# Exps of an attention stage moved to VectorE and GpSimd, and an earlier fetch of row maxima

## The chip, the core and the metric

The kernel runs on one NeuronCore of a Trainium2 chip. The core has five engines that run in parallel, each its own stream of instructions in order: TensorE (PE in the profile) multiplies matrices, with weight loads shown as PEld; ScalarE (ACT) evaluates functions such as exp; VectorE (DVE) does elementwise work and reductions; GpSimd (POOL) does elementwise work and issues some DMAs; SyncE (SP) issues DMAs alone. Operands lie in SBUF, 128 partitions wide; TensorE writes to PSUM, eight banks. Engines wait for each other on semaphores. The metric is device time in microseconds (us), lower is better.

## The reference, cut to what matters

Four graph layers on x (3327 x 128) and a 3327 x 3327 matrix adj, each of the form x = x + layer(relu(layernorm(x)), adj). The change is in layer 0, an attention with 128 heads of 8 elements each. Both encodings are adj, so that adj is added twice:

```python
q = (x @ Wq.T).reshape(d, n, h)          # d = 128 heads, n = 3327, h = 8
k = (x @ Wk.T).reshape(d, n, h)
v = (x @ Wv.T).reshape(d, n, h)
a = jnp.einsum('dnh,dmh->dnm', q, k) * scale
a = a + spatial_encoding + edge_encoding # both are adj
a = jax.nn.softmax(a, axis=2)
out = jnp.einsum('dnm,dmh->dnh', a, v)
```

There are 128 x 3327 x 3327 exps. The other three layers are products with adj or its transpose, with small elementwise work.

## The kernel before, in words

The attention stage takes the time from about 515 to 10,478 us of the profiled span. It holds the scores transposed: keys on partitions, queries along the free axis. The queries are cut into NC = 7 chunks of CW = 476 columns; the 128 heads into NG = 32 groups of four; the 3328 padded keys into NT = 26 tiles of 128, taken two at a time as NQ = 13 pairs (q = 0 to 12). One unit `u` is one (chunk, group, pair). Four heads of 26 tiles, less some hand work, are what a group asks of ScalarE.

A pair occupies two PSUM banks of the seven of `S`, one per tile (r = 0 "even" and r = 1 "odd"). `seed` (L660, VectorE) copies the half of the shifted adjacency that the pair needs into each bank. `scores` (L666, TensorE) then adds k.q of the first head, and for each next head k.q minus that of the head before, in place: adj and the shift are put in once for four heads. `exps` (L678 and L681, ScalarE) reads the bank after each head and writes exp(2 S) to SBUF tiles `e0` to `e3`. Where a pair's banks lie side by side, one ScalarE instruction takes both (952 columns, "wide", L678); in one pair of seven they don't, and two of 476 are used (L681). `values` (L719, TensorE) multiplies the exps by v, with a column of ones for the softmax's denominator, into the bank `po`, four heads side by side.

The order is written out by hand, in program order per engine, by the loop over slots `i`. A slot is one exp of one head of one pair; four slots make a unit, and heads are staggered: head j of unit u is in slot 4u + 3j. At odd slots TensorE gets the scores of the next two slots and then the value products of one tile of an earlier unit: the tile in place p of a group (0 to 25) comes in slot 2p + 11 from the group's start. `seed` of the odd bank comes at slots with i % 4 = 1, of the even bank at i % 4 = 2. After a bank's last exp, its next seed may start.

For pairs 0, 4 and 8 (`by_hand`), the second tile's exp of head 0 isn't ScalarE's: VectorE evaluates a polynomial (`hand_exp`, L692 to L703), in nine steps spread over four units by the queue `by_vector`. `heads_of` puts the result later into the order of the value products.

GpSimd, in order, does these in each group: the DMAs that store `po`'s copy (L727 on VectorE, L731 on GpSimd, in pair 2 or 3 of the next group), then at pair 4 the six negations of the next group's q (`negate_q`, L576), the copy of the next v (`spread_v`, L586) and a check copy `all_here` (L590). These wait for the next group's loads, which SP issues at pair 1: `load_qk` (L564, L566, L568; 40 DMAs) and `load_v` (L581).

Beside this runs the preparation of later chunks. Each 128 x 128 column block of adj ("square") is loaded in four parts, transposed by VectorE in two halves a part (`turn`, L293; at pairs 7 and 11), reduced to row maxima (`largest`, L297), gathered to DRAM (`gather`, L312, four small DMAs), fetched back in another layout (`back`, L317), combined by VectorE into a bound (`finish`, L321 to L323, at pair 7), stored (L300), and shifted on GpSimd by 13 subtractions (`shift`, L307), one a unit. A square takes seven groups: parts in the groups with g % 7 = 1 to 4, gather to spread in g % 7 = 5, shifts in 6 and 0. There are 22 such squares. `plan_squares` sets these units. SP executes gather, `back` and the loads in the order of the program; before, `back` comes at pair 3, after the loads.

The adjacency tiles of a chunk sit in the pool `e_adj` and those of the next are loaded during the last group of a chunk.

Of the kernel before, what the change touches and what calls it, by code (L numbers as in the profile page):

```python
# [10 lines left out]
F32 = mybir.dt.float32  # L11
# [4 lines left out]
I32 = mybir.dt.int32  # L16
AF = mybir.ActivationFunctionType
ALU = mybir.AluOpType
# [4 lines left out]
P = 128  # L23
N = 3327
D = 128
H = 8
HD = D * H
NT = 26
NP = NT * P
NQ = NT // 2  # L30
# [5 lines left out]
NC = 7  # L36
CW = 476
# [11 lines left out]
EXP_C = (753.2197875976562, 522.0919799804688, 180.93934631347656, 41.8090705871582, 7.287807941436768)  # L49
EXP_LAST = 0.0013276338577270508  # L50
EXP_BITS = 117 + 0.3594970703125
LOG2_E2 = 2.8853900817779268
EXP_LEAST = -110.0
# [27 lines left out]
def width_of(c):  # L81

    return min(CW, N + 1 - c * CW)
# [8 lines left out]
def gnn_kernel(ctx: ExitStack, tc: tile.TileContext, x, adj, Wq, Wk, Wv, Wo, embed, layer,  # L92
# [442 lines left out]

    with tc.tile_pool(name="e1", bufs=1) as e1, tc.tile_pool(name="e_adj", bufs=30) as e_adj, \
            tc.tile_pool(name="e2", bufs=2) as e2, tc.tile_pool(name="e_e", bufs=1) as e_e, \
            tc.tile_pool(name="e_t", bufs=1) as e_t, tc.tile_pool(name="e_h", bufs=1) as e_h, \  # L540
            tc.tile_pool(name="e_ps", bufs=1, space=PSUM) as e_ps:


# [71 lines left out]
        with tc.If(loose < 1), tc.manual_schedule():  # L615
# [10 lines left out]
            pairs = [(c, g, q) for c in range(NC) for g in range(NG) for q in range(NQ)]  # L626
            n = len(pairs)
            adj_of, shift_of, v_of, e_of, here = {}, {}, {}, {}, {}
            by_vector = deque()

# [23 lines left out]
            def bank(u, r):  # L654
                return S[:, banks(u)[r], :width_of(pairs[u][0])]
# [17 lines left out]
            def exps(u, j):  # L673
                w, (even, odd) = width_of(pairs[u][0]), banks(u)
                e = e_of[u, j] = e_e.tile([P, 2, CW], F32, name=f"e{j}", bufs=(5, 4, 3, 2)[j])
                hand = j == 0 and by_hand(u)
                if even > odd and not hand:
                    touch(u, (0, 1), nc.scalar.activation(e[:, :, :w], S[:, odd:even + 1, :w], AF.Exp, scale=2.0))  # L678
                    return
                for r in range(1 if hand else 2):  # L680
                    touch(u, [r], nc.scalar.activation(e[:, 1 - r, :w], bank(u, r), AF.Exp, scale=2.0))  # L681

            def by_hand(u):

                return 0 <= u < n and pairs[u][2] in (0, 4, 8)

            def hand_exp(u):

# [13 lines left out]
                yield  # L702
                nc.vector.scalar_tensor_tensor(e, e, EXP_C[0], power.bitcast(F32), op0=ALU.add, op1=ALU.mult)  # L703

            def heads_of(u, r):


                first = (u, r)
                if by_hand(u) and r == 1:
                    first = (u + 1, 0)  # L710
                elif by_hand(u - 1):
                    first = (u, 1) if r == 0 else (u - 1, 1)
                return [first] + [(u, r)] * 3

            def values(u, r):
                c, g, q = pairs[u]
                w, k = width_of(c), c * NG + g
                for j, (v, of) in enumerate(heads_of(u, r)):
                    nc.tensor.matmul(po[32 * j:32 * j + H + 1, :w], VA[k % 2][:, 2 * pairs[v][2] + of, j, :],  # L719
                                     e_of[v, j][:, 1 - of, :w], start=(q == 0 and r == 0),  # L720
                                     stop=(q == NQ - 1 and r == 1))

            def store(u):
                c, g, q = pairs[u]
# [8 lines left out]
            def loads(u):  # L733

                c, g, q = pairs[u]
                k = c * NG + g
                if k + 1 < NC * NG:
                    nxt = divmod(k + 1, NG)
                    if q == 1:
                        load_qk(*nxt)  # L740
                        v_of[k + 1] = load_v(*nxt)
                    if q == 4:
                        negate_q(*nxt)
                        spread_v(*nxt, v_of.pop(k + 1))
                        here[k + 1] = all_here(*nxt)
                if c + 1 < NC and (g, q) == (0, 0):
                    plan_squares(c)
                if g == NG - 1 and c + 1 < NC:
                    if q == 0:
                        shift_of[c + 1] = load_shift(c + 1)  # L750
                        adj_of[c + 1] = []
                    while len(adj_of[c + 1]) < min(NT, 2 * q + 6):
                        adj_of[c + 1].append(load_adj(c + 1, len(adj_of[c + 1]), shift_of[c + 1]))


# [2 lines left out]
            def plan(u, f, *a):  # L758
                behind.setdefault(u, []).append((f, a))

            def plan_squares(c):
                for k, s in enumerate(range(squares_of(c), squares_of(c + 1))):
                    sq, u = Square(e_t, s), (c * NG + 7 * k + 1) * NQ
                    for j in range(4):
                        plan(u, sq.load, j)
                        plan(u + 7, sq.turn, j, 0)
                        plan(u + 11, sq.turn, j, 1)
                        plan(u + 12, sq.largest, j)
                        u += NQ
                    for k, f in ((0, sq.gather), (3, sq.back), (7, sq.finish), (8, sq.store), (10, sq.spread)):  # L770
                        plan(u + k, f)
                    for k in range(NQ):
                        plan(u + NQ + 5 + k, sq.shift, 2 * k, 2 * k + 2)
                    plan(u + 2 * NQ + 6, sq.store, shifted_by_tile)
# [15 lines left out]
            for i in range(-4, 4 * n + 15):  # L790
                u, j = in_slot(i)
                if 0 <= u < n:
                    exps(u, j)
                at = i % 4
                if i == -4:
                    seed(0, 0)
                if at == 0 and by_hand(i // 4):
                    by_vector.append(hand_exp(i // 4))
                if at == 0 and by_vector:
                    for k in range(2 if by_hand(i // 4) else 3):  # L800
                        if by_vector and next(by_vector[0], True):
                            by_vector.popleft()
                if at == 0 and i > 0:
                    for f, a in behind.pop(i // 4, ()):
                        f(*a)
                if at == 1 and (i + 3) // 4 < n:
                    seed((i + 3) // 4, 1)
                u = (i - 14) // 4
                if at == 2 and 0 <= u < n and pairs[u][2] == NQ - 1:
                    store(u)  # L810
                if at == 2 and (i + 6) // 4 < n:
                    seed((i + 6) // 4, 0)
                if at % 2:
# [409 lines left out]
```

## Time and profile before

| What | Value |
|---|---|
| median of 3 runs | 11,431.28 us (11,428.13 to 11,438.58) |
| profiled execution: its time | 11,439.36 us |
| profiled execution: its span | 11,437.2 us |
| granted TensorE clock | 0.969 of full |
| busy in the stage (515.6 to 10,478 us, 9,962.4 us): TensorE, ScalarE | 9,783.0, 9,762.0 us |
| busy in the stage: VectorE, GpSimd | 7,634.5, 1,813.3 us |

The span is the time from the first to the last instruction of the profiled execution; the execution's own time is 2.2 us longer. Durations in the profile are of that one execution. A line of instructions reads: source line, engine, operation, output and inputs with their shapes, count, then busy time and mean of one in ns, then the idle time of the engine just before it and what ended it. A line of waits reads: who waited for whom, us in total, times, longest. A line of the timeline reads: start, length in us, engine, line, operation, and in brackets the idle time before it. ScalarE's instructions overlap: a wide exp is listed with 1,180 ns, while the next starts earlier.

### The profile page before, as it was taken

The page shows a single profiled execution, that of the slowest core. Times are in us where ns is not written, and L with a number is a line of the kernel's source. Part 1 is how long each engine was busy: PE and PEld are TensorE (multiplying, and loading weights), DVE is VectorE, ACT ScalarE, POOL GpSimd, SP SyncE. Part 2 cuts the span into 40 slices and gives each one's busy share as a digit, 9 for nine tenths or more (in the row PEclk, how much of TensorE's full clock was granted, in tenths as well). Part 3 has the DMA queues.
Part 4 walks back from the last instruction along what each step waited for, and adds up shares of the span by engine and source line. Part 5 has one row for each costly group of instructions (what it writes and reads, how often), then busy time and mean ns, then how long its engine had stood idle before and what let it go on. Part 6 is the DMA issues. An engine that isn't in the chain of part 4 may idle for free.

```text
span 11437.2 us, 205561 instructions
## 1 busy us (share of the span) xinstructions
PE 10803.1 (94%) x72980; PEld 3659.9 (32%) x72980; DVE 8338.7 (73%) x13563; ACT 10117.7 (88%) x13718; POOL 2054.9 (18%) x3417
## 2 busy tenths in 40 slices
PE   4599999999999999999999999999999999998779
PEld 2133333333333333333333333333333333334444
DVE  5577777777777777777777777777777777777633
ACT  3599999999999999999999999999999999996220
POOL 5211211111112111121111111121111111111000
PEclk7799999999999999999999999999999999999889
DMA  8755555555555555555555555555554544444447
GB/s 244 247 94 98 92 96 113 98 94 91 100 109 100 95 90 92 103 99 95 89 100 110 97 92 97 95 116 94 91 99 85 108 79 84 82 81 126 155 176 272
DMA packets 732443, 1280.87 MB, mean 112 GB/s; under 512 B 190462, under 2 KB 607750, under 8 KB 714908
## 3 DMA queue, kind: packets, MB, share of 16 engines
q1 hardware_dynamic: 689528, 1138.10, 51.2%
q0 software_dynamic: 41888, 129.51, 3.8%
q8 instruction: 591, 9.68, 0.4%
q14 instruction: 436, 3.57, 0.1%
HBM read 1082.90 MB, written 184.09 MB: 111 GB/s over the span
## 4 chain that ended last, share of the span: by engine, by line
ACT 42%; PE 37%; issue 7%; DMA 5%; DVE 4%; SPq 1%; POOL 0%; DVEq 0%; POOLq 0%; ACTq 0%
ACT e L678 35%; PE po L719 17%; PE S L666 14%; ACT e L681 7%; PE pu L1016 5%; DMA QS<-qS_d 2%; DMA KT<-kS_d 2%; DVE S L660 1%; DVE e L701 1%; DMA four<-rowmax_d 1%; PE pu L968 0%; SPq L564 0%; DVE OS L727 0%; DMA ot<-oT_d 0%; DVE xs L1003 0%
## 5 line engine op out<-in xcount | busy, mean ns | idle before, releaser
L678 ACT ACTIVATE e<-S 128x952 f32<-128x952 f32 (+1 forms) x9408 | 8761.8, 1180 | 172.0 <-PE S L666 170.2
L719 PE MATMUL po<-e,VA 128*9 128x476 f32 (+1 forms) x46592 | 5767.2, 567 | 19.4 <-DVE OS L727 1.1
L660 DVE COPY S<-a 128x476 f32<-128x476 f32 (+1 forms) x5824 | 3814.1, 655 | 1994.3 <-ACT e L678 1521.1
L666 PE MATMUL S<-QS,KT 64*128 64x476 f32 (+1 forms) x23296 | 4869.7, 452 | 188.9 <-DVE S L660 178.3
L666 PEld LDWEIGHTS S<-QS,KT 64*128 64x128 f32 x23296 | 2435.1, 184 | 5333.6 <-issue 1642.7
L681 ACT ACTIVATE e<-S 128x476 f32<-128x476 f32 (+1 forms) x3808 | 2432.5, 791 | 36.8 <-PE S L666 36.3
L701 DVE SCALAR_TENSOR_TENSOR e<-e,h 128x476 f32<-128x476 f32 (+1 forms) x2016 | 1395.6, 692 | 46.1
L731 POOL DMA_DIRECT2D oT_d<-OS x896 | 471.7, 532 | 4911.6 <-DVE OS L727 4828.1
L719 PEld LDWEIGHTS po<-e,VA 128*9 128x9 f32 x46592 | 691.2, 88 | 1586.8 <-issue 1495.1
L576 POOL TENSOR_SCALAR QS<-QS 32x476 fp32r<-32x476 f32 (+1 forms) x1344 | 853.4, 635 | 1368.9 <-DMA QS<-qS_d 724.9
L692 DVE TENSOR_SCALAR h<-S 128x476 f32<-128x476 f32 (+1 forms) x672 | 438.5, 653 | 82.0 <-PE S L666 10.9
L701 DVE SCALAR_TENSOR_TENSOR e<-h 128x476 f32<-128x476 f32 (+1 forms) x672 | 451.5, 672 | 0.0
L696 DVE TENSOR_TENSOR h<-h,h 128x476 f32<-128x476 f32 (+1 forms) x672 | 440.4, 655 | 0.0
L703 DVE SCALAR_TENSOR_TENSOR e<-e,h 128x476 f32<-128x476 f32 (+1 forms) x672 | 435.8, 649 | 0.0
L134 ACT COPY uT<-pu 128x494 f32<-128x494 f32 (+1 forms) x12 | 6.6, 546 | 427.3 <-PE pu L1016 427.3
L586 POOL COPY VA<-VR 128x832 f32<-128x832 f32 x224 | 198.8, 888 | 966.7 <-DMA VR<-v_d 687.5
L1016 PE MATMUL pu<-strip,h 128*128 128x494 f32 (+2 forms) x728 | 293.9, 564 | 38.9 <-ACT h L949 38.9
L694 DVE TENSOR_SCALAR h<-h 128x476 f32<-128x476 f32 (+1 forms) x672 | 306.2, 456 | 23.2
L1016 PE MATMUL pu<-strip,y 128*128 128x494 f32 (+2 forms) x728 | 295.5, 568 | 29.0 <-DVE y L1003 18.0
L698 DVE TENSOR_SCALAR h<-h 128x476 int32<-128x476 f32 (+1 forms) x672 | 288.1, 429 | 22.9
L307 POOL TENSOR_TENSOR cols<-cols,on_all 128x256 f32<-128x256 f32 x286 | 249.4, 906 | 0.2
L293 DVE STREAM_TRANSPOSE cols<-rows 128x416 f32<-128x416 f32 x208 | 203.7, 984 | 21.6 <-DMA rows<-in_adj_dram 14.1
(186 smaller groups left out, 2445.8 us busy)
## 6 DMA issues: line engine op xcount, KB each, us to landing
KT<-kS_d SPq DMA_DIRECT2D x1792, 208.0 KB
KT<-kS_d SPq DMA_DIRECT2D x1792, 104.0 KB
VR<-v_d SPq DMA_DIRECT2D x224, 416.0 KB
strip<-adjT POOLq DMA_DIRECT2D x39, 1663.5 KB, 7.3
strip<-adjT SPq DMA_DIRECT2D x36, 1663.5 KB
QS<-qS_d SPq DMA_DIRECT2D x3072, 14.9 KB
QS<-qS_d SPq DMA_DIRECT2D x1536, 29.8 KB
adjT<-cols SPq DMA_DIRECT2D x26, 1664.0 KB
```

The costliest lines, as they stand in the source:

```text
L576: nc.gpsimd.tensor_scalar(QS[b][r0:r0 + 32, j + 1, :w], QS[b][r0:r0 + 32, j, :w].bitcast(F32), -1.0, 0.0, op0=ALU.mult, op1=ALU.add)
L660: touch(u, [r], nc.vector.tensor_copy(bank(u, r), adj_of[c][2 * q + r][:, :w]))
L666: x = nc.tensor.matmul(bank(u, r), KT[b][64 * r:64 * r + 64, max(0, j - 1), q * P:(q + 1) * P], QS[b][64 * r:64 * r + 64, j, :w], start=Fa ...
L678: touch(u, (0, 1), nc.scalar.activation(e[:, :, :w], S[:, odd:even + 1, :w], AF.Exp, scale=2.0))
L681: touch(u, [r], nc.scalar.activation(e[:, 1 - r, :w], bank(u, r), AF.Exp, scale=2.0))
L692: touch(u, [1], nc.vector.tensor_scalar(f, bank(u, 1), LOG2_E2, EXP_LEAST, op0=ALU.mult, op1=ALU.max))
L696: nc.vector.tensor_tensor(f, f, whole, op=ALU.subtract)
L701: nc.vector.scalar_tensor_tensor(e, f if k == 4 else e, EXP_C[k], f, op0=ALU.add, op1=ALU.mult)
L703: nc.vector.scalar_tensor_tensor(e, e, EXP_C[0], power.bitcast(F32), op0=ALU.add, op1=ALU.mult)
L719: nc.tensor.matmul(po[32 * j:32 * j + H + 1, :w], VA[k % 2][:, 2 * pairs[v][2] + of, j, :], e_of[v, j][:, 1 - of, :w], start=(q == 0 and r ...
L731: nc.gpsimd.dma_start(oT_d[:, d * N + c * CW:d * N + c * CW + w], o[32 * j:32 * j + H + 1, :w])
L1016: nc.tensor.matmul(pu[c][:, :w], y[:m, t, :], s[:m, c * AW:c * AW + w], start=(t == 0), stop=(t == NT - 1))
```

## The change

1. `back` (L317 before) is planned one unit after `gather` and not three, so that it stands on SP's queue ahead of the 41 loads of q, k and v and not behind them. Both halves of `turn` come at pair 11; one was at pair 7.
2. A new kind of exp, `pool_exp`: in pair 2 of all groups, and in pair 6 of the groups with g % 7 in (0, 5, 6) and of all groups of the last chunk, head 0's second tile is taken from ScalarE. VectorE scales and rounds (two operations) and makes the power of two (one, a unit later); GpSimd evaluates the polynomial in ten operations, in four steps over four units. The step of a unit is issued ahead of that unit's loads and negations, so the fourth step of pair 2, issued at pair 5, stands on GpSimd's queue behind the negations, the copy of v and the check copy of pair 4. The scratch tiles p0 (f), p1 (whole), p2 and p3 have one buffer each, the result two.
3. `order_of` takes the place of `heads_of`: the tiles of head 0 are sorted so that a hand result is used 17 slots after its unit's first slot or later, and a GpSimd result 25 slots. For pair 2 this is place 11 (slot 33), for pair 6 place 19 (slot 49).
4. The hand exps' steps per unit are 3, or 1 in a unit with a `pool_exp` and 2 in the one after.
5. `e_adj` has 28 buffers and not 30, and the next chunk's tiles are loaded up to 2q + 4 and not 2q + 6.

```diff
-    with tc.tile_pool(name="e1", bufs=1) as e1, tc.tile_pool(name="e_adj", bufs=30) as e_adj, \
+    with tc.tile_pool(name="e1", bufs=1) as e1, tc.tile_pool(name="e_adj", bufs=28) as e_adj, \
...
+            tc.tile_pool(name="e_p", bufs=1) as e_p, \
...
-                hand = j == 0 and by_hand(u)
+                hand = j == 0 and (by_hand(u) or by_pool(u))
...
+            def by_pool(u):
+                if not 0 <= u < n:
+                    return False
+                c, g, q = pairs[u]
+                return q == 2 or q == 6 and (c == NC - 1 or g % 7 not in (1, 2, 3, 4))
+
+            def pool_exp(u):
+                w = width_of(pairs[u][0])
+                f, whole, f2, b = (e_p.tile([P, CW], F32, name=f"p{i}")[:, :w] for i in range(4))
+                e = pool_of[u] = e_p.tile([P, CW], F32, name="ep", bufs=2)
+                e, power = e[:, :w], whole.bitcast(I32)
+                touch(u, [1], nc.vector.tensor_scalar(f, bank(u, 1), LOG2_E2, EXP_LEAST, op0=ALU.mult, op1=ALU.max))
+                nc.vector.tensor_scalar(whole, f, ROUNDER, ROUNDER, op0=ALU.add, op1=ALU.subtract)
+                pool = nc.gpsimd
+                pool.tensor_tensor(f, f, whole, op=ALU.subtract)
+                yield
+                pool.tensor_tensor(f2, f, f, op=ALU.mult)
+                pool.tensor_scalar(e, f, 1.0, EXP_C[4], op0=ALU.mult, op1=ALU.add)
+                nc.vector.tensor_scalar(power, whole, EXP_BITS, 2.0 ** 23, op0=ALU.add, op1=ALU.mult)
+                pool.tensor_tensor(e, e, f2, op=ALU.mult)
+                yield
+                pool.tensor_scalar(b, f, EXP_C[3], EXP_C[2], op0=ALU.mult, op1=ALU.add)
+                pool.tensor_tensor(e, e, b, op=ALU.add)
+                pool.tensor_tensor(e, e, f2, op=ALU.mult)
+                yield
+                pool.tensor_scalar(b, f, EXP_C[1], EXP_C[0], op0=ALU.mult, op1=ALU.add)
+                pool.tensor_tensor(e, e, b, op=ALU.add)
+                pool.tensor_tensor(e, e, power.bitcast(F32), op=ALU.mult)
...
-            def heads_of(u, r):
...
+            def order_of(u0):
+                order, left = [], list(range(NT))
+                for k in range(NT):
+                    t = next(t for t in left if 2 * k + 11 >= 4 * (t // 2) + (
+                        2 if t % 2 == 0 else 17 if by_hand(u0 + t // 2) else 25 if by_pool(u0 + t // 2) else 2))
+                    order.append(t)
+                    left.remove(t)
+                return order
...
-                    while len(adj_of[c + 1]) < min(NT, 2 * q + 6):
+                    while len(adj_of[c + 1]) < min(NT, 2 * q + 4):
...
-                        plan(u + 7, sq.turn, j, 0)
+                        plan(u + 11, sq.turn, j, 0)
                         plan(u + 11, sq.turn, j, 1)
...
-                    for k, f in ((0, sq.gather), (3, sq.back), (7, sq.finish), (8, sq.store), (10, sq.spread)):
+                    for k, f in ((0, sq.gather), (1, sq.back), (7, sq.finish), (8, sq.store), (10, sq.spread)):
...
+                if at == 0 and by_pool(i // 4):
+                    by_gpsimd.append(pool_exp(i // 4))
+                if at == 0 and by_gpsimd and next(by_gpsimd[0], True):
+                    by_gpsimd.popleft()
                 if at == 0 and by_vector:
-                    for k in range(2 if by_hand(i // 4) else 3):
+                    for k in range(1 if by_pool(i // 4) else 2 if by_pool(i // 4 - 1) else 3):
```

More of the change, by code (lines that the diff above doesn't have):

```diff
@@ L628, in gnn_kernel @@
             adj_of, shift_of, v_of, e_of, here = {}, {}, {}, {}, {}
-            by_vector = deque()
+            by_vector, by_gpsimd, pool_of = deque(), deque(), {}
             def banks(u):
@@ L703, in hand_exp @@
                 nc.vector.scalar_tensor_tensor(e, e, EXP_C[0], power.bitcast(F32), op0=ALU.add, op1=ALU.mult)
-            def heads_of(u, r):
[L708 to L713, printed above, removed]
+            def order_of(u0):
[6 more added lines that the diff above has]
+                return order
             def values(u, r):
@@ L717, in values @@
                 w, k = width_of(c), c * NG + g
[L718 to L721, printed above, removed]
+                for j in range(4):
+                    t = order_of(u - q)[2 * q + r] if j == 0 else 2 * q + r
+                    v, of = u - q + t // 2, t % 2
+                    e = pool_of[v] if of and j == 0 and by_pool(v) else e_of[v, j][:, 1 - of, :]
+                    nc.tensor.matmul(po[32 * j:32 * j + H + 1, :w], VA[k % 2][:, t, j, :], e[:, :w],
+                                     start=(q == 0 and r == 0), stop=(q == NQ - 1 and r == 1))
             def store(u):
```

## The prediction, made before the changed kernel ran

> **What bounds the kernel now.** The page first: busy time and the groups of the attention stage, which fills 515 to 10,478 us of the span.
>
> ```profile
> PE 10803.1 (94%) x72980; PEld 3659.9 (32%) x72980; DVE 8338.7 (73%) x13563; ACT 10117.7 (88%) x13718; POOL 2054.9 (18%) x3417
> L678 ACT ACTIVATE e<-S 128x952 f32<-128x952 f32 (+1 forms) x9408 | 8761.8, 1180 | 172.0 <-PE S L666 170.2
> L660 DVE COPY S<-a 128x476 f32<-128x476 f32 (+1 forms) x5824 | 3814.1, 655 | 1994.3 <-ACT e L678 1521.1
> ```
>
> ScalarE is never idle in the last chunk, and TensorE's 9s in the slices hide waits: its weight loads for the scores stand 1551.7 and 1024.0 us for the two exp lines. VectorE's seed of an odd bank starts 0.03 us after the exp that frees the bank (median), its score matmul 0.06 us after the seed, and the exp 0.2 us after that. So ScalarE's exps set the pace, in a loop in which a late VectorE has nothing to hide behind. A usual group lasts 43.79 us (median gap of the L727 copies), a slot 0.84 us.
>
> Next the waits, for what stops VectorE and GpSimd.
>
> ```profile
> DVE b L321 <- DMA four<-rowmax_d: 154.6, 22, 8.3
> POOL QS L576 <- DMA QS<-qS_d: 724.9, 343, 8.5
> POOL VA L586 <- DMA VR<-v_d: 687.5, 157, 8.4
> ```
>
> 22 times VectorE stands for the row maxima, and in nearly every group GpSimd stands for loads. The timeline of one such stall, VectorE and then SP's queue (start, length):
>
> ```profile
> 5961.52 0.65 DVE L703 SCALAR_TENSOR_TENSOR e<-e,h 128x476 f32<-128x476 f32 x1
> 5969.05 0.16 DVE L321 TENSOR_REDUCE b<-four 128x1 f32<-128x4 f32 x1 [6.88 <-DMA four<-rowmax_d]
> 5969.81 1.40 DVE L660 COPY S<-a 128x476 f32<-128x476 f32 x2
> 5965.52 0.39 SPq L581 DMA_DIRECT2D VR<-v_d  x1
> 5965.95 0.51 SPq L317 DMA_DIRECT2D four<-rowmax_d  x1
> ```
>
> The fetch is issued last, behind all loads of q, k and v, and lands 3 us later. In the next group, GpSimd and then VectorE around pair 6:
>
> ```profile
> 6003.09 2.62 POOL L576 TENSOR_SCALAR QS<-QS 32x476 fp32r<-32x476 f32 x4
> 6011.39 0.59 POOL L576 TENSOR_SCALAR QS<-QS 32x476 fp32r<-32x476 f32 x1 [1.86 <-DMA QS<-qS_d]
> 6016.16 0.88 POOL L586 COPY VA<-VR 128x832 f32<-128x832 f32 x1 [4.18 <-DMA VR<-v_d]
> 6016.98 0.18 POOL L590 COPY seen<-KT 128x3 f32<-128x3 f32 x1
> 6008.84 1.42 DVE L660 COPY S<-a 128x476 f32<-128x476 f32 x2
> 6010.16 2.31 DVE L701 SCALAR_TENSOR_TENSOR e<-e,h 128x476 f32<-128x476 f32 x3
> ```
>
> GpSimd is done with the loads at 6017.2; VectorE begins pair 6 at 6010.2. That order decides the forecast. The prices, by tile (min/median/max ns):
>
> ```profile
> L602 POOL TENSOR_TENSOR a<-a,shb x52: 258/968/1614, 449.0 to 1904.1; 128x476 f32<-128x476 f32 x26, 128x36 f32<-128x36 f32 x26
> L698 DVE TENSOR_SCALAR h<-h x672: 405/408/1299, 457.8 to 10458.6; 128x476 int32<-128x476 f32 x144, 128x472 int32<-128x472 f32 x24
> ```
>
> **What the skill says.** The Trainium skill, "PSUM — Partial Sum Buffer", section "Engine vs sequencer instructions": the queues of ScalarE, VectorE and GpSimd are strictly first in, first out. The trace agrees: spread_v, issued at pair 4, stands 4.18 us for v, and nothing passes it. "SBUF — State Buffer", section "Who interferes with whom": a GpSimd operation that reads SBUF and a VectorE one with two SBUF inputs, or in a fast mode, lock each other out for a whole instruction. It agrees in size: L698, usually 408 ns, took up to 1,299.
>
> **Part 1, the fetch.** The 22 groups with a stall lie 192.3 us above 22 x 43.79. Issued two pairs earlier, ahead of the 41 loads, the fetch lands long before pair 7: -192 us. Its cost: SP now waits for the four gather DMAs before the loads, some 2 us of landing (estimate from the 3 us above), so in those groups the loads, and GpSimd with them, end 2 us later. If the cover fails, the gain is 150; it can't pass 200.
>
> **Part 2, fewer exps for ScalarE.** 224 groups lose the second half of pair 2; 6 x 13 + 32 = 110 also that of pair 6: 334 halves. ScalarE starts lie 837 ns apart after a wide exp and 443 after a narrow one (medians, 9,300 to 10,300 us). Six pairs of seven turn a wide exp into a narrow one (0.394), the seventh drops a narrow one (0.443): 0.40 x 334 = -134 us. VectorE takes on 0.65 + 0.41 + 0.41 us an exp (L692, L694, L698), 491 us in all, inside the 1,616 us that it stood for ScalarE in the stage; uncovered, that would be +491.
>
> **Part 3, the wait that the change makes.** GpSimd's order is fixed: steps 1 to 3 of pair 2's exp, then the six L576 negations, spread_v and the check L590, all waiting for loads, and only then step 4. I measure from the end of pair 2's second seed. The check ends at 21.6 us in the median and 22.3 in the mean of 222 groups (10th to 90th percentile 20.5 to 25.1). Steps 1 to 3 don't delay it: 4 stores (2.1), 1.2 + 3.0 + 3.0 of arithmetic and 3.5 of negations end by about 16.5, and v lands at 20.6. Step 4 is one scalar and two tensor-tensor operations: 0.58 (L576's median, though of 32 partitions) + 1.19 + 1.19 (L602's uncontended 128x476; its longest, 1.61, is the upper bound) = 2.96.
>
> In the 110 groups, VectorE comes to the first operation of pair 6's exp at 15.3. It overwrites f and whole, which have one buffer each and which step 4 of pair 2 still has to read. So f waits for step 4's first operation and whole for its last: mean 22.3 + 0.4 (the 2 us in 22 of 110) + 2.96 = 25.7. Then whole 0.41 and a hand step 0.65, and the seed of pair 7 starts at 26.7 where it started at 16.4: 10.3 us late. Queued behind it are all later seeds; TensorE's scores and the exps wait for them. What such lateness costs is in the trace: in the 22 stalls the seed came 6.9 us late (26.6 for 19.7) and the group grew by 8.7. Add the same 1.8: 12.1 x 110 = +1,331 us. Low end 9.9, without refilling; high end 14.5, with slow GpSimd operations.
>
> In the other 114 groups only TensorE waits: its value matmul of pair 2 stands at 22.6, the result is there at 22.3 + 2.96 + 0.1 = 25.4. Of the 2.8, TensorE's own waiting for ScalarE hides 0.44 (2,576 us over 5,824 half pairs): 2.4 x 114 = +274. Between 1 and 4.
>
> **Part 4, the shared port.** One exp is 7 x 1.19 + 3 x 0.58 = 10 us of GpSimd. The groups with 11 shifts in a row (9.25 us) last 44.48 us against 43.79: 0.7 lost. VectorE will be fuller, so I take 1.0, between 0.2 and 3. For pair 2 it falls before the waits of part 3 and is inside them; pair 6 pays it: 110 x 1.0 = +110.
>
> The turn moved to pair 11 puts two 0.98 us transposes beside 1.42 of seeds, 3.38 of a pair's 3.37: nothing, covered by no hand step being there; without that cover 88 x 1 us. Fewer adj buffers and the new matmul order: nothing, the counts stay and the chunk's tiles are fetched a whole group ahead; a missed prefetch would cost the six chunk changes some microseconds each.
>
> Sum: -192 - 134 + 1,331 + 274 + 110 = +1,389. On the profiled 11,439.4 (span 11,437.2) that is 12,828; the median of the runs stands 8 lower: 12,820.
>
> **Rivals.** (a) Faster: GpSimd gives the buffers back in time. Then parts 1 and 2 remain with 0.2 of contention, 11,431 - 326 + 67 = 11,170. It needs the check at 12.4 (15.3 - 2.96); no tenth of the groups is under 20.3. Against it also: the loads are SP's chain of issues, which the change doesn't shorten. 0.08. (b) The wait comes, but half is hidden, the refill costs nothing and the port little: 5 x 110 + 0.5 x 114 + 67 - 326 = +348, 11,780. For it: pair 6's wait starts later if pair 2's contention had slowed the group. 0.09. (c) The port is the main cost, 3 us for each exp of pair 6 and 4 for pair 2: 12,820 + 220 + 182, and 110 x 0.84 for two GpSimd operations at 1.61: 13,310. For it, L698 at three times its length; against, the 0.7. 0.06. (d) The fetch isn't quicker after all, since SP waits for the gather: part 1 gives nothing, 13,010. 0.05, inside the forecast's case.
>
> **How the numbers follow.** The forecast's case has 0.75: 110 x 9.9 + 114 - 326 + 22 gives +900, 12,330; 110 x 14.5 + 114 x 4 + 330 - 276 gives +2,100, of which the worst ends don't meet, so 12,330 to 13,250. The range goes down to 12,000 to take in part of (b). Faster, by over 0.2% (about what can be told from no change): (a), 0.08; same 0.02, where (a) meets a port cost near 1 us; slower 0.90.
>
> **What would show it.** Right: in the waits, L321 gone; a new VectorE wait for GpSimd at the first two operations of the exp, some 110 times of 7 to 10 us; groups of 54 to 56 us next to ones of 46; GpSimd's last three operations directly behind L590; ScalarE below 85% in the stage. Wrong: L590 ending before VectorE's pair 6, no such wait, groups all near 43 us; or L698 and L701 at twice their length without long waits, which is (c).

## The result, and the profile after

The changed kernel takes 13,103.62 us (median of 4 runs, 13,097.86 to 13,111.38); the kernel before took 11,434.93 us beside it (4 runs, 11,428.13 to 11,439.66). The ratio is 1.146, with a 95% interval of 1.144 to 1.148. The forecast was 12,820 us, so the direction and most of the size came true, and 284 us were missing.

Here and below, a group's length is the time from one copy of `po` (L763 now, L727 before) to the next. The 110 groups that have a new exp in pair 6 too are shown without the first and the last of the stage, which have no full gap or no loads behind them; the other 114 have the exp of pair 2 alone. A square is gathered in 22 groups.

| Groups | before, us | after, us | in the forecast |
|---|---|---|---|
| 114 with pair 2's exp alone, mean | 43.88 | 47.06 | +2.0 |
| 108 with pair 6's too, mean | 45.55 (43.89 with the fetch alone, below) | 57.34 | +12.3 on a group without a stall |
| of these, the 22 in which a square is gathered, median | 52.65 | 63.07 | |
| the last chunk's, median | 43.46 | 54.93 | |

The page of the kernel after, its busy times and the groups of instructions that the change touched (the columns as before):

```profile
PE 11291.2 (86%) x72980; PEld 3616.8 (28%) x72980; DVE 9724.3 (74%) x14565; ACT 10176.3 (78%) x13669; POOL 5871.1 (45%) x6757
L679 ACT ACTIVATE e<-S 128x952 f32<-128x952 f32 (+1 forms) x9123 | 8369.3, 1025 | 1530.9 <-PE S L667 1488.5
L661 DVE COPY S<-a 128x476 f32<-128x476 f32 (+1 forms) x5824 | 3801.4, 653 | 1269.8 <-ACT e L679 855.0
L705 POOL TENSOR_TENSOR p<-p,p 128x476 f32<-128x476 f32 (+1 forms) x334 | 508.6, 1523 | 3944.3 <-DVE p L703 3944.3
L702 DVE TENSOR_SCALAR p<-S 128x476 f32<-128x476 f32 (+1 forms) x334 | 218.2, 653 | 785.9 <-POOL p L716 755.4
L729 DVE TENSOR_TENSOR h<-h,h 128x476 f32<-128x476 f32 (+1 forms) x672 | 712.4, 1060 | 23.3
L734 DVE SCALAR_TENSOR_TENSOR e<-h 128x476 f32<-128x476 f32 (+1 forms) x672 | 669.9, 997 | 0.0
```

Three things stand in it. The wide exps (L679), which waited 172.0 us in all before, now wait 1,530.9. The first operation of the new exp (L702) has GpSimd's step 4 (L716) in front of it. And two operations of the *old* hand exps, whose code did not change, take 1,060 and 997 ns, where the same lines took these before:

```profile
L701 DVE SCALAR_TENSOR_TENSOR e<-h 128x476 f32<-128x476 f32 (+1 forms) x672 | 451.5, 672 | 0.0
L696 DVE TENSOR_TENSOR h<-h,h 128x476 f32<-128x476 f32 (+1 forms) x672 | 440.4, 655 | 0.0
```

So there are two costs, not one.

**The wait.** VectorE's waits of the kernel after (who waited for whom, total, times, longest):

```profile
DVE S L661 <- ACT e L679: 855.0, 799, 19.1
DVE p L702 <- POOL p L716: 755.4, 109, 14.4
DVE p L703 <- POOL ep L718: 206.3, 110, 1.9
```

One instance in the timeline, first GpSimd, then VectorE (start, length, idle time before):

```profile
6063.10 0.88 POOL L587 COPY VA<-VR 128x832 f32<-128x832 f32 x1 [3.96 <-DMA VR<-v_d]
6063.92 0.19 POOL L591 COPY seen<-KT 128x3 f32<-128x3 f32 x1
6064.07 0.59 POOL L716 TENSOR_SCALAR p<-p 128x476 f32<-128x476 f32 x1
6064.74 1.19 POOL L717 TENSOR_TENSOR ep<-ep,p 128x476 f32<-128x476 f32 x1
6066.01 1.20 POOL L718 TENSOR_TENSOR ep<-ep,p 128x476 f32<-128x476 f32 x1
```

```profile
6050.13 1.40 DVE L661 COPY S<-a 128x476 f32<-128x476 f32 x2
6064.69 0.65 DVE L702 TENSOR_SCALAR p<-S 128x476 f32<-128x476 f32 x1 [13.16 <-POOL p L716]
6067.24 0.41 DVE L703 TENSOR_SCALAR p<-p 128x476 f32<-128x476 f32 x1 [1.90 <-POOL ep L718]
6067.56 0.65 DVE L734 SCALAR_TENSOR_TENSOR e<-e,h 128x476 f32<-128x476 f32 x1
6068.12 1.41 DVE L661 COPY S<-a 128x476 f32<-128x476 f32 x2
```

v lands, the check L591 ends at 6064.1, step 4 follows directly, L702 starts when L716 is done and L703 when L718 is done. The seeds of the next pair (6068.12) come 18 us after the last ones. This is the forecast's picture, line by line, in a group where a square is gathered.

**The port.** The busy time of each engine in two successive pairs, of a group that has *no* pair 6 exp and no wait for loads (each stretch runs from the seed of one odd bank to the next; length, then busy time and count by engine):

```profile
core 0: us, PE busy (x) PEld busy (x) DVE busy (x) ACT busy (x) POOL busy (x), PEclk, DMA share, GB/s
3902.54:3906.66 4.12, 4.12 (x33) 1.20 (x25) 3.84 (x6) 4.12 (x8) 3.88 (x5) 1.00 1.07 143
3906.66:3911.19 4.53, 3.71 (x25) 1.01 (x24) 4.39 (x7) 3.82 (x5) 4.20 (x5) 1.00 0.90 125
```

and in the same two pairs of the same group before:

```profile
3442.45:3445.15 2.70, 2.70 (x24) 0.97 (x16) 2.38 (x5) 2.70 (x6) 2.05 (x4) 1.00 1.01 140
3445.15:3449.03 3.88, 3.88 (x35) 1.10 (x32) 2.84 (x5) 3.88 (x6) 0.58 (x1) 1.00 0.98 139
```

In the second stretch VectorE was busy for 2.84 of 3.88 us and ScalarE throughout. Now VectorE is busy for 4.39 of 4.53, GpSimd for 4.20, and ScalarE stands for 0.71. VectorE has become the bound there, and the timeline of this stretch shows with what:

```profile
3905.19 1.54 DVE L729 TENSOR_TENSOR h<-h,h 128x476 f32<-128x476 f32 x1
3906.66 1.40 DVE L661 COPY S<-a 128x476 f32<-128x476 f32 x2
3907.97 0.77 DVE L731 TENSOR_SCALAR h<-h 128x476 int32<-128x476 f32 x1
3908.66 1.65 DVE L734 SCALAR_TENSOR_TENSOR e<-h 128x476 f32<-128x476 f32 x1
```

```profile
3904.75 1.48 POOL L710 TENSOR_TENSOR ep<-ep,p 128x476 f32<-128x476 f32 x1
3908.55 1.25 POOL L714 TENSOR_TENSOR ep<-ep,p 128x476 f32<-128x476 f32 x1
```

L710 ends at 3906.23 and L729 0.50 us later, L714 ends at 3909.80 and L734 0.51 us later: each looks like an operation that was held until GpSimd's was through. In this profile L729 takes 0.65 us in the mean where no GpSimd instruction overlaps it and 1.39 where one does; L734 with these operands 0.65 and 1.52. The copies L661 take what they always took. In the 114 groups the seed of pair 7 comes 19.34 us after the origin that the prediction uses, against 16.40 before; nearly the whole growth of these groups (3.18 us) is there already. Two of the 114 are apart. The last group of chunk 0 went from 43.9 to 67.7 us: ahead of the new exp's first operation an adjacency shift (L603) stands on GpSimd's queue for its load, 27.6 us, and VectorE's L709 waits 21.1 us for what is behind it. In group 18 of chunk 5 (52.5 to 64.5 us) TensorE waits 18 us for the new exp's result. Without these two the mean went from 43.80 to 46.72.

### The profile page after: what moved, and what is told of

It reads as the page before. It is cut to its first block, busy times and chain, and to the rows that moved or that the text cites. A ratio compares the mean times of both kernels' runs of the same rounds, so it can differ in the third digit from the quotient of the medians.

```text
span 13096.0 us, 210640 instructions
## 1 busy us (share of the span) xinstructions
PE 11291.2 (86%) x72980; PEld 3616.8 (28%) x72980; DVE 9724.3 (74%) x14565; ACT 10176.3 (78%) x13669; POOL 5871.1 (45%) x6757
## 5 line engine op out<-in xcount | busy, mean ns | idle before, releaser
L679 ACT ACTIVATE e<-S 128x952 f32<-128x952 f32 (+1 forms) x9123 | 8369.3, 1025 | 1530.9 <-PE S L667 1488.5
L667 PE MATMUL S<-QS,KT 64*128 64x476 f32 (+1 forms) x23296 | 5150.1, 452 | 1283.7 <-DVE p L702 665.7
L756 PE MATMUL po<-e,VA 128*9 128x476 f32 (+1 forms) x45924 | 5963.5, 585 | 32.5 <-DVE OS L763 9.4
L661 DVE COPY S<-a 128x476 f32<-128x476 f32 (+1 forms) x5824 | 3801.4, 653 | 1269.8 <-ACT e L679 855.0
L682 ACT ACTIVATE e<-S 128x476 f32<-128x476 f32 (+1 forms) x4044 | 2278.7, 641 | 276.9 <-PE S L667 273.2
L705 POOL TENSOR_TENSOR p<-p,p 128x476 f32<-128x476 f32 (+1 forms) x334 | 508.6, 1523 | 3944.3 <-DVE p L703 3944.3
L734 DVE SCALAR_TENSOR_TENSOR e<-e,h 128x476 f32<-128x476 f32 (+1 forms) x2016 | 1541.5, 765 | 34.7
L702 DVE TENSOR_SCALAR p<-S 128x476 f32<-128x476 f32 (+1 forms) x334 | 218.2, 653 | 785.9 <-POOL p L716 755.4
L729 DVE TENSOR_TENSOR h<-h,h 128x476 f32<-128x476 f32 (+1 forms) x672 | 712.4, 1060 | 23.3
L734 DVE SCALAR_TENSOR_TENSOR e<-h 128x476 f32<-128x476 f32 (+1 forms) x672 | 669.9, 997 | 0.0
L736 DVE SCALAR_TENSOR_TENSOR e<-e,h 128x476 f32<-128x476 f32 (+1 forms) x672 | 559.9, 833 | 23.1
L725 DVE TENSOR_SCALAR h<-S 128x476 f32<-128x476 f32 (+1 forms) x672 | 439.1, 653 | 114.4 <-PE S L667 52.4
L710 POOL TENSOR_TENSOR ep<-ep,p 128x476 f32<-128x476 f32 (+1 forms) x334 | 485.3, 1453 | 27.9
L717 POOL TENSOR_TENSOR ep<-ep,p 128x476 f32<-128x476 f32 (+1 forms) x334 | 431.5, 1292 | 27.9
L731 DVE TENSOR_SCALAR h<-h 128x476 int32<-128x476 f32 (+1 forms) x672 | 435.0, 647 | 0.0
L714 POOL TENSOR_TENSOR ep<-ep,p 128x476 f32<-128x476 f32 (+1 forms) x334 | 421.1, 1261 | 26.2
L713 POOL TENSOR_TENSOR ep<-ep,p 128x476 f32<-128x476 f32 (+1 forms) x334 | 409.3, 1225 | 27.9
L718 POOL TENSOR_TENSOR ep<-ep,p 128x476 f32<-128x476 f32 (+1 forms) x334 | 410.0, 1228 | 26.2
```

The lines of the kernel that those rows point to most:

```text
L661: touch(u, [r], nc.vector.tensor_copy(bank(u, r), adj_of[c][2 * q + r][:, :w]))
L667: x = nc.tensor.matmul(bank(u, r), KT[b][64 * r:64 * r + 64, max(0, j - 1), q * P:(q + 1) * P], QS[b][64 * r:64 * r + 64, j, :w], start=Fa ...
L705: pool.tensor_tensor(f, f, whole, op=ALU.subtract)
L729: nc.vector.tensor_tensor(f, f, whole, op=ALU.subtract)
L734: nc.vector.scalar_tensor_tensor(e, f if k == 4 else e, EXP_C[k], f, op0=ALU.add, op1=ALU.mult)
```

## The experiments

Ratios are to the kernel before, run beside each kernel on the same chip (medians of 11,457, 11,466 and 11,460 us for the three sets of kernels). Differences of ratios are turned into us with the 11,435 of the result; an interval of 0.002 is 23 us.

### The fetch alone

```diff
 (the kernel before)
-for k, f in ((0, sq.gather), (3, sq.back), (7, sq.finish), ...
+for k, f in ((0, sq.gather), (1, sq.back), (7, sq.finish), ...
```

> The kernel before with the fetch of the row maxima (back) one unit after gather, nothing else. Theory (the fetch is worth the 22 stalls): VectorE's wait for the maxima gone, the 22 groups of 52.5 us back to 44 to 45, 11,240 us, between 11,230 and 11,290. Rival (SP's wait for the gather ahead of the loads gives the gain back): 11,380 to 11,440.

Measured: 11,261.61 us, ratio 0.9828 [0.9811, 0.9844]: -197 us. The 22 groups with a gather fell from 52.16 us in the mean to 43.86, and the wait L321 is gone. The price is on SP's queue; first the kernel before, then this one:

```profile
SPq L317 <- DMA rowmax_d<-rm: 1.1, 1, 1.1
```

```profile
SPq L317 <- DMA rowmax_d<-rm: 139.6, 37, 6.8
```

SP now stands for the gather ahead of the loads, about 6.3 us in each of 22 groups, and the check in these groups ends at 30.8 us from the origin (the end of pair 2's second seed, as in the prediction) instead of 26.4. In this kernel TensorE waits for the check only twice, 5.2 us in all, so it costs next to nothing. In the changed kernel something does.

### Pair 2 alone, without pair 6

```diff
 (the changed kernel)
-return q == 2 or q == 6 and (c == NC - 1 or g % 7 not in (1, 2, 3, 4))
+return q == 2
```

> The changed kernel with the GpSimd exp in pair 2 alone, none in pair 6. Theory (two costs, the wait of pair 6 for step 4 and the shared port): no VectorE wait for GpSimd at the first operation of the exp, but all groups at 46 to 47.5 us like those without an exp in pair 6 now, VectorE's three-operand lines still 20 to 60% longer: 11,930 to 12,000 us. Rival (the wait is the only cost): groups of 43.4 us, 11,150 us.

Measured: 12,181.77 us, ratio 1.0631 [1.061, 1.0653], about 200 us over the expectation. Most groups last 46 to 48 us, 46.75 in the mean. The 22 gather groups last 56.72, some 10 us more, which makes 22 x 10 = 220 us: the rest. What stands there is TensorE. The view of the tile `ep`, who waited for the result:

```profile
who waited for it (us, times):
  PEld po L756: 345.7, 141
  PE po L756: 289.7, 85
```

In these groups the late fetch of v pushes the check to 31.0 us from the origin, and step 4 behind it, so the wait exists also without pair 6, and longer than the cover that the other groups have.

### Two buffers for f and whole

```diff
-f, whole, f2, b = (e_p.tile([P, CW], F32, name=f"p{i}")[:, :w] for i in range(4))
+f, whole, f2, b = (e_p.tile([P, CW], F32, name=f"p{i}", bufs=(2, 2, 1, 1)[i])[:, :w] for i in range(4))
```

with 26 buffers in `e_adj` in place of 28, for the space, and loads up to 2q + 2.

> The changed kernel with two buffers each for f and whole (p0, p1), the adj pool cut to 26 buffers to make room. Theory (VectorE waits on GpSimd's queue, which waits for loads, wherever it first needs it): the wait of 8.7 us at the first operation of pair 6's exp goes, but the power of two a unit later overwrites whole only after GpSimd's first operation of that exp, which stands behind step 4: there VectorE waits 4 to 6 us instead, groups of 53 to 55 us, 12,650 to 12,800 us. Rival (the single buffers are the whole cause): no wait left, 12,200 us.

Measured: 13,052.6 us, ratio 1.1391 [1.1369, 1.1414], a gain of 0.7% where 2 to 4 were expected. VectorE's waits of this kernel:

```profile
DVE p L709 <- POOL p L705: 861.6, 111, 20.9
```

L702 and L703 no longer wait. The wait has gone one unit further: L709 makes the power of two in place of `whole`, which GpSimd's first operation L705 still has to read, and L705 stands on GpSimd's queue behind the same loads. The gap between the odd seeds of pairs 7 and 8 is now 11.98 us, as it was 11.92 between pairs 6 and 7. The buffer was only the place where VectorE noticed that GpSimd was late; the queue is the cause.

### The loads' work later on GpSimd's queue

```diff
 (the changed kernel; negate_q, spread_v and all_here)
-if q == 4:
+if q == 8:
```

> The changed kernel with the negations, the copy of v and the check copy issued at pair 8 and not 4, behind all four steps of pair 2's exp. Theory: GpSimd never stands for loads ahead of a step, so both waits go and only the shared port is left, some 3 us for pair 2 and 2.5 for pair 6 less 0.4 each: groups of 46.5 and 48.5 to 49.5 us, 12,050 to 12,300 us. Rival (what looks like the port is the wait's echo): 11,150 us.

Measured: 12,412.22 us, ratio 1.0833 [1.0811, 1.0854]: 0.0627 or 717 us less than the changed kernel, with the same exps and the same GpSimd work. The waits of L702 for L716 are down from 755.4 to 5.2 us, L703's from 206.3 to 60.9. Groups with pair 6 last 50.84 us in the mean (57.34 in the changed kernel), the others 47.14. So the wait was real, and worth 6.5 us in each of the 110 groups. Yet 8.3% remain without it, more than expected.

### Pair 2 alone, and no wait

```diff
 (the changed kernel)
-return q == 2 or q == 6 and (c == NC - 1 or g % 7 not in (1, 2, 3, 4))
+return q == 2
...
-if q == 4:
+if q == 8:
```

> The changed kernel with the GpSimd exp in pair 2 alone and the negations, the copy of v and the check copy at pair 8, so that nothing waits for GpSimd's loads: what is left is the price of one GpSimd exp beside VectorE. Theory (shared port, 3 us an exp against 0.4 saved): groups of 46.5 to 47 us, 11,860 to 11,960 us, VectorE's operations with two SBUF inputs still 20 to 60% longer in the mean. Rival (what pair 2 alone cost before was the wait for its result): groups of 43.5 to 44 us, 11,200 us.

Measured: 12,015.18 us, ratio 1.0479 [1.0448, 1.0509]. The groups last 47.1 us, the gather groups as the rest (46.93). But for the last group of chunk 0 (66.8 us, as above) no engine waits for the new exp behind loads any more, and still each of 224 exps costs 0.0651 x 11,435 / 224 = 3.3 us over the kernel with the fetch alone. The page:

```profile
L679 ACT ACTIVATE e<-S 128x952 f32<-128x952 f32 (+1 forms) x9216 | 8468.4, 1055 | 658.0 <-PE S L667 624.5
L729 DVE TENSOR_TENSOR h<-h,h 128x476 f32<-128x476 f32 (+1 forms) x672 | 651.3, 969 | 23.3
L734 DVE SCALAR_TENSOR_TENSOR e<-h 128x476 f32<-128x476 f32 (+1 forms) x672 | 665.8, 991 | 0.0
```

The three-operand lines are still half as long again as before, and ScalarE waits 658 us. It could be the reading of GpSimd, or just that GpSimd and VectorE have more to do and more signals to exchange; the next two runs tell these apart.

### Half of GpSimd's operations, and fills in their place

The first kernel leaves out five of the ten polynomial operations of an exp (its values are no exps then):

```diff
 (pair 2 alone and no wait)
-pool.tensor_tensor(e, e, f2, op=ALU.mult)
...
-pool.tensor_scalar(b, f, EXP_C[3], EXP_C[2], op0=ALU.mult, op1=ALU.add)
-pool.tensor_tensor(e, e, b, op=ALU.add)
...
-pool.tensor_scalar(b, f, EXP_C[1], EXP_C[0], op0=ALU.mult, op1=ALU.add)
-pool.tensor_tensor(e, e, b, op=ALU.add)
```

> As pair2_late, with five of GpSimd's ten operations left out (the middle of the polynomial: two of the scalar operations, the two additions and one product), so that the exps of pair 2 are not exps any more; VectorE's three operations stay. Theory (the cost goes with GpSimd's time at the port): half of the 3 us goes, groups of 45.0 to 45.8 us, 11,550 to 11,680 us. Rival (VectorE is simply overfull with its 1.5 us more): groups stay at 46.5 us or more, 11,850 us.

Measured: 11,604.65 us, ratio 1.012 [1.0091, 1.015]. Groups of 45.0 us in the median, where ten operations gave 46.8.

The second leaves the polynomial out altogether and puts 17 fills of `ep` with ones in its place, so that GpSimd is as busy as before, and writes, but doesn't read:

```diff
 (pair 2 alone and no wait; likewise in the other steps: 2, 5, 5 and 5 fills)
-pool.tensor_scalar(b, f, EXP_C[1], EXP_C[0], op0=ALU.mult, op1=ALU.add)
-pool.tensor_tensor(e, e, b, op=ALU.add)
-pool.tensor_tensor(e, e, power.bitcast(F32), op=ALU.mult)
+for k in range(5):
+    pool.memset(e, 1.0)
```

> As pair2_late, with GpSimd's ten operations replaced by 17 fills of the result with a constant, which write SBUF and read nothing (the exps of pair 2 are left out; VectorE's three operations stay). Theory (the read side of the port is what VectorE's operations with two SBUF inputs wait for): L729, L734 and L736 of the hand exps back to 645 to 660 ns in the mean, the fast one-input ones perhaps longer, groups of 43.6 to 44.8 us, 11,200 to 11,450 us. Rival (any GpSimd work beside VectorE, or VectorE overfull): 46 us or more, 11,850 us.

Measured: 11,304.27 us, ratio 0.9859 [0.983, 0.9887]. Groups of 43.9 us. The page (lines lie two higher than in the changed kernel: L727 here is L729 there, L732 is L734):

```profile
L679 ACT ACTIVATE e<-S 128x952 f32<-128x952 f32 (+1 forms) x9216 | 8491.0, 1084 | 78.4 <-PE S L667 36.4
L709 POOL MEMSET ep<- 128x476 f32 (+1 forms) x1120 | 589.8, 527 | 51.6
L727 DVE TENSOR_TENSOR h<-h,h 128x476 f32<-128x476 f32 (+1 forms) x672 | 457.3, 680 | 23.3
L732 DVE SCALAR_TENSOR_TENSOR e<-h 128x476 f32<-128x476 f32 (+1 forms) x672 | 444.9, 662 | 0.0
```

17 x 0.52 = 8.8 us of GpSimd's time in each group, beside the same VectorE operations, and these are back at 680 and 662 ns (655 and 672 before). ScalarE waits 78 us and not 658. So GpSimd's being busy is not what costs.

The fills also take away the signals between VectorE and GpSimd, since they read nothing of VectorE's. Signals would show as waits, however, and reading as longer instructions. The first line of each page, with ten operations and then with fills:

```profile
PE 10863.0 (90%) x72980; PEld 3556.9 (30%) x72980; DVE 9383.8 (78%) x14235; ACT 10145.3 (84%) x13686; POOL 4774.3 (40%) x5657
PE 10760.4 (95%) x72980; PEld 3595.5 (32%) x72980; DVE 8659.3 (77%) x14235; ACT 10084.4 (89%) x13686; POOL 4027.9 (36%) x7225
```

VectorE executes the same 14,235 instructions in both, and is busy with them for 724.5 us more. That is the whole difference in time: 1.0479 - 0.9859 = 0.0620, or 709 us, 3.2 us an exp. And with ten operations L729 takes 654 ns in the mean where no GpSimd instruction overlaps it and 1,484 where one does, with the same signals in both cases. So it is the operations that read.

### The changed kernel with the fetch as it was

```diff
 (the changed kernel)
-for k, f in ((0, sq.gather), (1, sq.back), (7, sq.finish), ...
+for k, f in ((0, sq.gather), (3, sq.back), (7, sq.finish), ...
```

> The changed kernel with the fetch of the row maxima back at three units after gather, behind the loads. Theory (VectorE already stands at pair 6 until GpSimd is past the same loads, so the fetch is covered; and without SP's wait for the gather the loads of the 22 groups end 2 us earlier): 13,040 to 13,110 us, no wait of L321 over 2 us. Rival (the fetch is worth 192 us here too): 13,290 us.

Measured: 13,089.06 us, ratio 1.1415 [1.1382, 1.1448]; the changed kernel has 1.146 [1.144, 1.148]. The earlier fetch, worth 197 us alone, is worth nothing here that can be measured. No wait L321 is left in this kernel either: `finish` lies at pair 7, and by the time that VectorE gets past its wait in pair 6 the maxima are there. On the other hand the check in the gather groups ends at 27.1 us from the origin and not at 28.8, and these groups last 61.19 us in the mean and not 62.95.

### What an exp less is worth to ScalarE, and what VectorE's part costs

The fetch alone once more, as a base for the other two:

> The kernel of fetch_only once more, as the base of the next two on the same chip: 0.983 of before.

Measured: 11,261.23 us, ratio 0.9827 [0.981, 0.9843].

On it, pair 2's exp of the second tile is left out and the value product reads the first tile's in its place, so that ScalarE's half is gone and nothing replaces it:

```diff
 (the fetch alone)
-hand = j == 0 and by_hand(u)
+hand = j == 0 and (by_hand(u) or pairs[u][2] == 2)
...
-e_of[v, j][:, 1 - of, :w], ...
+e_of[v, j][:, 1 if j == 0 and pairs[v][2] == 2 else 1 - of, :w], ...
```

> The kernel of fetch_only, with head 0's exp of pair 2's second tile left out (the value product reads the first tile's instead): ScalarE has 0.40 us less in each of 224 groups and no engine has more. Theory of the prediction's part 2 (ScalarE's exps set the pace): groups of 43.4 us, 90 us under fetch_again. Rival (the loop of exp, seed and scores sets the pace, and ScalarE waits where the half is missing): groups of 43.7 us or more, within 20 us of fetch_again.

Measured: 11,209.47 us, ratio 0.9782 [0.9765, 0.9798], 52 us less than the base: between the two expectations, 0.23 us for each of 224 halves and not 0.40. The median group goes from 43.8 to 43.6 us. Where the other 0.17 go isn't shown.

Last, the changed kernel's order with pair 2 alone, no wait, VectorE's three operations, and one fill in place of the polynomial (left out):

```diff
 (pair 2 alone and no wait)
-pool.tensor_tensor(f, f, whole, op=ALU.subtract)
+pool.memset(e, 1.0)
 (and GpSimd's nine other operations left out)
```

> As pair2_late_write with one fill of the result in place of 17, so that nearly nothing is left on GpSimd: the changed order, ScalarE's exp of pair 2 gone, VectorE's three operations (1.5 us) more; the exps of pair 2 are left out. Theory (VectorE's added work takes ScalarE's saving away, not GpSimd's writes): groups of 43.7 to 43.9 us as in pair2_late_write, within 25 us of fetch_again. Rival (the fills cost it): 90 us under fetch_again.

Measured: 11,316.89 us, ratio 0.9876 [0.9859, 0.9892]: 56 us over the base, somewhat more than expected, and 107 over the kernel in which the exp is simply left out, 0.48 us an exp. The three operations take 1.47 us of VectorE. Together with the new order of the value products, the turn and the `adj` buffers, which this run can't keep apart, they take more than the exp gave. So the exchange would lose some 0.25 us an exp even if GpSimd worked for nothing.

### The sum

Each step is a difference of two ratios above:

| Step | Ratios | us |
|---|---|---|
| fetch earlier | 1 to 0.983 | -197 |
| pair 2's exps, nothing waiting for the loads | 0.983 to 1.048 | +744 (3.3 an exp) |
| pair 6's exps, nothing waiting for the loads | 1.048 to 1.083 | +405 (3.7 an exp) |
| the wait behind the loads | 1.083 to 1.146 | +717 (6.5 in each of 110 groups) |
| the whole | 1 to 1.146 | +1,669 |

With another order of the steps some values would be others: the fetch as the last step is worth nothing.

The fastest kernel that computes all is the one with the fetch alone. It beats both, with 0.983 both times that it was run.

## Why the prediction was right, and where it wasn't

**The mechanism of the wait: right, shown.** Step 4 behind L591, VectorE behind step 4, the seeds behind VectorE, 109 times, for 6.9 us in the mean at L702 and 1.9 at L703: all in the lines above. The seed of pair 7 was forecast at 26.7 us from the origin and came at 26.86 in the mean. "Groups of 54 to 56 us next to ones of 46", ScalarE "below 85%" (9,838 of 11,624 us, 84.6%) and the missing L321 came too.

**Its size: too large (Part 3).** The forecast put all 10.3 us of that seed's lateness down to the wait, and a refill of 1.8 on top. The trace agrees on the total, 10.5 us, but not on what it is made of. In the kernel with pair 2 alone the same seed comes at 19.02 in these groups, so 2.7 us were lost to the port before the wait began; the gap from pair 6 to 7 holds the other 7.9 (11.92 for 3.98). Part 3 had said that pair 2's contention falls inside the wait. That is so for the moment of the seed, but it means that the contention is what remains when the wait is taken away. Taken away, the wait was worth 6.5 us and not 12.1. Where the last 1.4 between 7.9 and 6.5 go wasn't tried.

**The other 114 groups: grew for another reason (Part 3, its end).** TensorE's value product was to wait 2.4 us a group, +274 us. Its matmuls wait for `ep` 64 us in all the 114 groups, its weight loads 93, partly at the same moments, and 18 of each are in one group. With pair 2 alone and no wait these groups are just as long (47.09 and 47.06 us). The working left out that the same contention moves TensorE's slot: 22.6 us plus the 2.9 that the seeds were late by then is 25.5, when the result, due at 25.4, is there. The groups still grew, by 3.18 us where 2.0 were forecast, and nearly all of that remains when nothing waits for the loads.

**The port: the term that failed (Part 4).** "I take 1.0, between 0.2 and 3", for pair 6 alone, +110. It is 3.2 us for an exp of pair 2, just outside the range. If pair 6's cost as much, which no run separates, all 334 exps make some +1,070 us (estimate, 334 x 3.2): more than the wait. The value was taken from the groups with 11 shifts in a row, which grow by 0.7. But growth is only what is left when VectorE's room is used up. Summed from the trace of before, the hand exps' instructions beside those 11 shifts take 2.1 us longer than where GpSimd does nothing, and VectorE had room for two thirds of it. Beside one exp of pair 2, where nothing waits, they take 3.6 us longer, and VectorE's three new operations, 1.47 us, want room as well. In the changed kernel pair 2's polynomial runs in pairs 2 to 5, and pair 4's hand exp, with its two operations of 1.5 to 1.7 us, lies in that stretch, where VectorE had 1 us to spare in 3.9. The Trainium skill, "SBUF — State Buffer", section "Who interferes with whom", names the pairs of operations that lock each other out, and the fills, which lock nobody out of a two-input operation, agree with that distinction (680 and 662 ns, where reading operations gave 969 and 991). The trace of before had the price of one such meeting, L698 at up to 1,299 ns, and the prediction quoted it and then took the growth of a group.

**ScalarE and VectorE (Part 2): signs right, cover wrong.** -0.40 an exp was -0.23, and VectorE's operations, "inside the 1,616 us that it stood for ScalarE", cost 0.48, with the new order of the value products in it. Why its waiting didn't cover them wasn't tried. Over 334 exps this is about +80 us where -134 was forecast.

**The fetch (Part 1): right alone, empty in this kernel.** -192 forecast, -197 measured. One of its 22 long groups was no fetch: in group 18 of chunk 5 TensorE waits 6.2 us for the check L590, and the group is long with the early fetch too (50.3 us for 52.5); that is 9 us of the 192. The 2 us of delay to the loads are 1.7 in the changed kernel (28.8 for 27.1 us) and 4.4 in the kernel with the fetch alone (30.8 for 26.4). But -192 was added to a sum in which every gather group waits in pair 6 for longer than the stall that was removed. Two waits in one place don't add.

So the total was near by luck, because two errors were opposed: waits of 717 us for a forecast 1,605, port, ScalarE and VectorE together +1,149 for a forecast -24. Rival (c), "the port is the main cost", had the price of the port right (3 to 4 us an exp), and put it on top of the full wait. Rivals (a) and (b) fell. Rival (d), 13,010, is near in time, and the reason it gave isn't what happened: the fetch is quicker, and its gain is covered.

## What to carry to other kernels

Before work is put on an idle in-order engine, look at what stands on its queue: part of the idle time here *was* the wait for loads, and what is issued behind it inherits it; a second buffer only moved the place where VectorE met it. Elementwise work that reads SBUF on GpSimd must be priced by what VectorE does at the same time, instruction by instruction, from what its instructions lose and the room there is to lose it in, and not from how much a group with room grew; here an exp whose removal from ScalarE was worth 0.23 us cost 3.2 us of the whole core. When two gains or waits end in the same place, test each in the presence of the other, as the fetch shows.

## What the runs showed of the hardware

**Reading, not working, is what VectorE and GpSimd contend for.** 17 fills in a group cost nothing that can be measured against a single one (0.9859 and 0.9876); ten reading operations cost 3.2 us, five of them 1.1 by the groups (45.0 for 43.9 us) and 1.3 by the ratios. GpSimd pays as well: a two-input operation of 1.19 us alone took, by line, 1.23 (L713) to 1.52 us (L705) in the mean, and the ten together 11.1 us for an estimated 10. VectorE's copies into PSUM (653 ns for 655) and TensorE's score matmuls (452 ns in both kernels) were untouched. Not only two-input operations grew: L731, with one input and an int32 result, took 647 ns in the mean for 429 before, and 427 beside fills. And fills aren't free for every operation: L725 there, the rounding with one input, took 537 ns, where with ten reading operations (as L727) it took 427.

**TensorE comes back from a wait at half clock.** The granted clock was 1.00 in the groups shown, but behind the long wait (the busy times by stretch, the same columns; then TensorE's timeline):

```profile
6060.00:6065.00 5.00, 0.00 (x0) 0.00 (x0) 0.31 (x1) 0.00 (x0) 1.81 (x4) 0.50 0.31 92
6065.00:6070.00 5.00, 4.33 (x17) 1.28 (x21) 3.00 (x6) 1.33 (x2) 4.32 (x4) 0.50 0.01 3
6070.00:6075.00 5.00, 4.83 (x28) 1.26 (x32) 4.72 (x8) 3.77 (x6) 4.62 (x6) 0.76 0.02 0
6075.00:6080.00 5.00, 4.78 (x36) 1.31 (x28) 4.83 (x7) 4.59 (x6) 4.51 (x4) 1.00 1.33 127
```

```profile
6051.44 0.98 PE L756 MATMUL po<-e,VA 128*9 128x476 f32 x8
6066.09 1.78 PE L756 MATMUL po<-e,VA 128*9 128x476 f32 x8
6069.92 1.77 PE L756 MATMUL po<-e,VA 128*9 128x476 f32 x8
6072.60 0.99 PE L756 MATMUL po<-e,VA 128*9 128x476 f32 x8
```

Eight value matmuls take 1.78 us in place of 0.98 until some 7 us after TensorE's work begins again at 6065.4, and ScalarE is busy for only 5.1 of these 10 us. The Trainium skill describes this ("TensorE: Matmul & The Clock Gate", "Part 1: The HAM clock gate"): a window of some 3.4 us without work halves the clock, a busy one restores it. The trace agrees on the half; the return took about twice that time here, with TensorE at first not fully busy. The prediction says nothing of it. The kernel before shows the same in the stall that the prediction quotes: a clock of 0.50 from 5970 to 5974 us and 1.00 from 5978. That a late seed costs more than its lateness, the "refill" of 1.8 us, may be in part this; it was not measured. The mean clock is lowest where the waits are most: 0.930 in the changed kernel, 0.962 where the loads' work comes later, 0.977 with the fetch alone.
